# The last layer norm of a two-layer transformer: all loads ahead of the stores, scaling shared, last store halved

## The chip, the cores and the metric

The kernel runs on one core of a Trainium2 chip. A core has engines that run their own instruction streams and meet at semaphores: TensorE (PE: matmuls), VectorE (DVE), ScalarE (ACT), GpSimd (POOL) and SyncE (SP), which here only issues DMAs. DMAs move data between the chip's memory (HBM) and the on-chip memory (SBUF); they run on 16 DMA engines, and the issuing engine goes on without waiting for them. The metric is the device time of one execution in microseconds (us), the median of several runs.

## What is computed

Two post-norm transformer layers over 4 x 1024 tokens of width 256: attention and a gated feed-forward layer, then causal attention and a mixture of experts. Each of the four parts is added to its input and normalised. Cut to its end:

```python
def _layernorm(x, axis=-1, eps=1e-05):
    m = jnp.mean(x, axis=axis, keepdims=True)
    v = jnp.var(x, axis=axis, keepdims=True)
    return (x - m) / jnp.sqrt(v + eps)
...
x = _layernorm(x + _L0_attn_ref(x, ...))
x = _layernorm(x + _L0_ffn_ref(x, ...))
x = _layernorm(x + _L1_attn_ref(x, ...))
x = _layernorm(x + _L1_ffn_ref(x, ...))     # the experts; this norm is the last stage
return x
```

The change concerns the last of these norms only.

## The kernel before

Tokens are taken 128 at a time (a tile: 128 partitions, 256 numbers each); there are `NT` = 32 tiles. The two attention layers and the first feed-forward layer run in an order written out by hand. After them the kernel is in the hands of a planner, which orders each engine's instructions by itself, within the dependencies.

The mixture of experts accumulates in HBM: `acc_d` holds, for every token, the input of the last norm. The copy expert, the constant experts and the residual are written there first; then each of 12 experts (`EM`) computes four chunks of 128 rows and GpSimd adds them to `acc_d` with an indirect DMA (L1430). Expert e waits for the additions of expert e-1.

The last stage works in eight groups of `GRP` = 4 tiles. For each group:

- SyncE loads the group `xo` from `acc_d` (L1459, 512 KB, 4 KB for each partition). The loads depend on the additions of the last expert (`added[EM]`). `xo` has eight buffers, so no load waits for a buffer.
- VectorE computes mean and variance of each tile: `bn_stats` (L1465) and `bn_aggr` (L1466) into `mvo`.
- GpSimd makes `rs` = (variance + 1e-5) to the power -0.5 for the four tiles (L95, L96, in `inv_std`) and `sho` = -mean x `rs` (L1469, L1470).
- `finish` scales the tiles and stores the group to `out` (L1455, SyncE, 512 KB in rows of 1 KB). Tiles up to number 26 are scaled on ScalarE (L1454, `Identity` with scale `rs` and bias `sho`), the last five on VectorE (`normalise`, L100: subtract the mean, multiply by `rs`).

`finish` of a group is called one group late, after the statistics of the next one (`done`). In the planned order SyncE issues the loads of groups 0 to 4, the stores of 0 and 1, the load of 5, the stores of 2, 3 and 4, the load of 6, the store of 5, the load of 7, and the stores of 6 and 7. SyncE issues in order: a store that waits for its scaling holds what stands behind it.

Of the kernel before, what the change touches and what calls it, by code (L numbers as in the profile page):

```python
# [13 lines left out]
AF = mybir.ActivationFunctionType  # L14
# [5 lines left out]
P = 128  # L20
B, S, C = 4, 1024, 256
N = B * S
NT = N // P
# [12 lines left out]
def postln_layers_kernel(ctx: ExitStack, tc: tile.TileContext, a: dict, out: bass.AP):  # L36
    nc = tc.nc
# [10 lines left out]
        out=mask_h, in_=mask_h, pattern=[[-1, P]], compare_op=ALU.is_ge, fill=NEG, base=0, channel_multiplier=1  # L48
# [18 lines left out]
        out=before, in_=before, pattern=[[1, P]], compare_op=ALU.is_gt, fill=0.0, base=0, channel_multiplier=-1  # L67
# [24 lines left out]
    def inv_std(work, var, n, name, rs=None):  # L92
        if rs is None:
            rs = work.tile([P, n], F32, tag="rstd", bufs=4, name=f"rs_{name}")
        nc.gpsimd.tensor_scalar(rs, var, 1e-5, None, ALU.add)  # L95
        nc.gpsimd.tensor_tensor(rs, rs, neg_half.to_broadcast([P, n]), ALU.pow)  # L96
        return rs

    def normalise(x, mean, rs):
        nc.vector.tensor_scalar(x, x, mean, rs, ALU.subtract, ALU.mult)  # L100

    with ExitStack() as main:
# [65 lines left out]
        for s in range(2):  # L168
            k = float(D0) ** -0.5 if s == 0 else 1.0
# [1172 lines left out]
        st, tu, lo = route(3, True)  # L1342
# [45 lines left out]
    for e in range(EM):  # L1388
# [34 lines left out]
        for c in range(ECH):  # L1423
            py = ps_av.tile([P, 512], F32, tag="av", name=f"py_{e}_{c}")
            for f in range(FF1 // P):
# [5 lines left out]
                out=acc_d,  # L1431
# [12 lines left out]


    GRP = 4
    done = []

    def finish(x, mv, rs, sh, t0):
        for t in range(GRP):  # L1450
            if t0 + t >= NT - 5:
                normalise(x[:, t], mv[:, t, 0:1], rs[:, t : t + 1])
            else:
                nc.scalar.activation(x[:, t], x[:, t], AF.Identity, bias=sh[:, t : t + 1], scale=rs[:, t : t + 1])  # L1454
        nc.sync.dma_start(out[t0 * P : (t0 + GRP) * P, :].rearrange("(t p) d -> p t d", p=P), x)  # L1455

    for t0 in range(0, NT, GRP):
        x = mo.tile([P, GRP, C], F32, tag="xo", bufs=NT // GRP, name=f"xo_{t0}")
        ins = nc.sync.dma_start(x, acc_rows[:, t0 : t0 + GRP, :])  # L1459
        for other in added[EM]:  # L1460
            tc.add_manual_dep(ins.ins, other.name, must, reason="all experts' rows")
        mv = mo.tile([P, GRP, 2], F32, tag="mvo", bufs=4, name=f"mvo_{t0}")
        for t in range(GRP):
            st = mo.tile([P, 6], F32, tag="bnst", bufs=4, name=f"st_o_{t0 + t}")
            nc.vector.bn_stats(st, x[:, t])  # L1465
            nc.vector.bn_aggr(mv[:, t], st)  # L1466
        rs = inv_std(mo, mv[:, :, 1], GRP, f"o_{t0}")
        sh = mo.tile([P, GRP], F32, tag="sho", bufs=4, name=f"sho_{t0}")
        nc.gpsimd.tensor_scalar(sh, mv[:, :, 0], -1.0, None, ALU.mult)  # L1469
        nc.gpsimd.tensor_tensor(sh, sh, rs, ALU.mult)  # L1470
        done.append((x, mv, rs, sh, t0))
        if len(done) > 1:
            finish(*done.pop(0))
    finish(*done.pop())


# [61 lines left out]
```

## Time and profile before

| | us |
|---|---|
| median of 3 runs (2526.11 to 2530.27) | 2527.09 |
| the profiled execution | 2529.43 |
| its span, first to last instruction | 2527.6 |
| the last stage in it, from the first load of `xo` to the end | 39.0 (2488.6 to 2527.6) |

Busy time in the whole span and in the last stage:

| engine | span, us | last stage, us | instructions in the last stage |
|---|---|---|---|
| TensorE | 2364.4 | 0 | 0 |
| VectorE | 1364.7 | 15.2 | 69 |
| ScalarE | 1024.8 | 13.6 | 27 |
| GpSimd | 729.4 | 13.3 | 32 |
| DMA engines, mean share | | 62% at 215 GB/s | 16 DMAs of 512 KB |

The groups of instructions of the last stage, as the profile lists them (line, engine, operation, out<-in with shapes, count; busy us and mean ns of one; idle time of the engine just before them, and what ended it):

```profile
L1454 ACT ACTIVATE xo<-xo,sho,rs_o 128x256 f32<-128x256 f32 x27 | 13.6, 586 | 32.2 <-DVE st_o L1465 24.9 <-POOL sho L1470 7.3
L1465 DVE BATCH_NORM_STATS2 st_o<-xo 128x6 f32<-128x256 f32 x32 | 12.3, 402 | 19.0 <-DMA xo<-acc_d 19.0
L96 POOL TENSOR_TENSOR rs_o<-rs_o,neg_half 128x4 f32<-128x4 f32 x8 | 8.3, 1037 | 0.0
L1466 DVE BATCH_NORM_AGGREGATE mvo<-st_o 128x2 f32<-128x6 f32 x32 | 5.1, 169 | 0.0
L100 DVE TENSOR_SCALAR xo<-xo,mvo,rs_o 128x256 f32<-128x256 f32 x5 | 1.8, 409 | 3.5 <-POOL rs_o L96 3.5
```

An instruction may start before the one ahead of it on its engine has ended, so the time from one start to the next is shorter than a mean duration. Times in the text are us from the start of the span.

### The profile page before, as it was taken

The page shows a single profiled execution, that of the slowest core. Times are in us where ns is not written, and L with a number is a line of the kernel's source. Part 1 is how long each engine was busy: PE and PEld are TensorE (multiplying, and loading weights), DVE is VectorE, ACT ScalarE, POOL GpSimd, SP SyncE. Part 2 cuts the span into 40 slices and gives each one's busy share as a digit, 9 for nine tenths or more (in the row PEclk, how much of TensorE's full clock was granted, in tenths as well). Part 3 has the DMA queues.
Part 4 walks back from the last instruction along what each step waited for, and adds up shares of the span by engine and source line. Part 5 has one row for each costly group of instructions (what it writes and reads, how often), then busy time and mean ns, then how long its engine had stood idle before and what let it go on. Part 6 is the DMA issues. An engine that isn't in the chain of part 4 may idle for free.

```text
span 2527.6 us, 36682 instructions
## 1 busy us (share of the span) xinstructions
PE 2364.4 (94%) x14452; PEld 1194.9 (47%) x14452; DVE 1364.7 (54%) x3157; ACT 1024.8 (41%) x2015; POOL 729.4 (29%) x1015
## 2 busy tenths in 40 slices
PE   6999999999999999999999999999999983999993
PEld 3343334444445543444445434445566442666662
DVE  6765654766657447787563677817435654111112
ACT  1355554545552445545424455461331331111122
POOL 5633623425114122454121320211110143122213
PEclk8999999999998999999989999999998985999996
DMA  3034212000000000001000000112000012444434
GB/s 92 29 119 135 84 59 83 1 27 1 1 1 27 1 1 1 23 26 51 31 1 1 1 1 1 48 33 86 1 1 1 1 51 68 108 111 103 117 72 141
DMA packets 79612, 109.89 MB, mean 43 GB/s; under 512 B 8784, under 2 KB 68432, under 8 KB 77776
## 3 DMA queue, kind: packets, MB, share of 16 engines
q1 hardware_dynamic: 54336, 80.48, 9.8%
q0 software_dynamic: 9984, 14.82, 3.0%
q10 hardware_dynamic: 15120, 12.27, 1.7%
q8 instruction: 113, 1.85, 0.3%
q14 instruction: 59, 0.48, 0.1%
HBM read 68.64 MB, written 38.90 MB: 43 GB/s over the span
## 4 chain that ended last, share of the span: by engine, by line
PE 85%; DVE 8%; DMA 3%; POOL 2%; ACT 1%; issue 1%; SPq 0%; ACTq 0%; DVEq 0%; POOLq 0%
PE sc L458 19%; PE av L476 10%; PE ph L1410 7%; PE py L1426 7%; PE gu L595 7%; PE mx L434 4%; PE sc L978 4%; PE mx L931 4%; PE p L898 4%; PE dn L611 3%; PE av L1015 3%; PE dn L1015 2%; DVE part L942 2%; PE qk L298 2%; PE ppa L559 2%; PE pt L425 2%
## 5 line engine op out<-in xcount | busy, mean ns | idle before, releaser
L437 DVE TENSOR_REDUCE part<-mx 128x1 f32<-128x512 f32 x1024 | 656.5, 685 | 344.3 <-PE mx L434 338.6
L467 ACT ACTIVATE pe<-sc 128x512 f32<-128x512 f32 x1024 | 554.1, 596 | 394.5 <-PE mx L434 341.8
L434 PE MATMUL mx<-kT,qT 32*128 32x512 f32 x2048 | 650.3, 644 | 6.0 <-DVE part L437 5.7
L458 PE MATMUL sc<-qT,kT 32*128 32x512 f32 x2048 | 616.3, 638 | 0.2 <-ACT pe L467 0.2
L458 PEld LDWEIGHTS sc<-qT,kT 32*128 32x128 f32 x2048 | 182.1, 183 | 223.8 <-issue 177.7
L476 PE MATMUL av<-pe,va 128*32 128x512 f32 x2048 | 272.8, 605 | 0.0
L942 DVE TENSOR_REDUCE part<-mx 128x1 f32<-128x512 f32 (+3 forms) x384 | 186.9, 550 | 152.3 <-PE mx L940 108.6
L434 PEld LDWEIGHTS mx<-kT,qT 32*128 32x128 f32 x2048 | 196.6, 185 | 52.7 <-DVE part L437 27.4
L989 ACT ACTIVATE pe<-sc 128x512 f32<-128x512 f32 (+3 forms) x384 | 157.6, 499 | 156.4 <-PE sc L978 156.1
L1410 PE MATMUL ph<-dmT,f 128*128 128x512 f32 x384 | 170.3, 602 | 4.4 <-DVE dmT L90 3.5
L1426 PE MATMUL py<-f,hTm 128*128 128x256 f32 x768 | 167.7, 379 | 0.0
L1418 ACT ACTIVATE hTm<-ph,b 128x512 f32<-128x512 f32 x96 | 60.8, 684 | 261.3 <-PE ph L1410 261.3
L992 POOL TENSOR_SCALAR_AFFINE_SELECT pe<-pe 128x256 f32<-128x256 f32 x128 | 51.7, 411 | 374.6 <-ACT pe L989 372.4
L1426 PEld LDWEIGHTS py<-f,hTm 128*128 128x128 f32 x768 | 145.9, 190 | 25.0 <-issue 5.7
L1430 POOL DMA_INDIRECT acc_d<-yo,dm x48 | 74.5, 1552 | 284.9 <-DVE yo L1428 238.8
L931 PE MATMUL mx<-kT,qT 32*128 32x512 f32 (+3 forms) x768 | 138.6, 593 | 8.5 <-DVE part L942 4.8
L356 POOL TENSOR_TENSOR ss<-ss,neg_half 128x16 f32<-128x16 f32 x48 | 138.7, 2907 | 0.5
L1427 DVE TENSOR_TENSOR yo<-py,b 128x256 f32<-128x256 f32 x48 | 20.4, 425 | 207.6 <-PE py L1426 207.6
L476 PEld LDWEIGHTS av<-pe,va 128*32 128x32 f32 x2048 | 40.3, 108 | 193.9 <-issue 183.9
L978 PE MATMUL sc<-qT,kT 32*128 32x512 f32 (+3 forms) x768 | 117.9, 546 | 1.7 <-DVE part L942 0.6
L1410 PEld LDWEIGHTS ph<-dmT,f 128*128 128x128 f32 x384 | 72.9, 192 | 94.9 <-issue 86.7
L595 PE MATMUL gu<-xTf,wg 128*128 128x256 f32 x384 | 107.7, 403 | 0.0
(357 smaller groups left out, 2938.0 us busy)
## 6 DMA issues: line engine op xcount, KB each, us to landing
f<-in_fc SPq DMA_DIRECT2D x14, 1024.0 KB, 5.0
f<-in_fc ACTq DMA_DIRECT2D x10, 1024.0 KB, 6.0
xink<-in_xT SPq DMA_DIRECT2D x32, 256.0 KB, 2.8
disp_d<-empty SPq DMA_DIRECT2D x12, 520.0 KB, 5.1
qk_d<-xs SPq DMA_DIRECT2D x6, 1024.0 KB, 3.9
xr<-qk_d SPq DMA_DIRECT2D x6, 1024.0 KB, 6.5
dm<-disp_d SPq DMA_DIRECT2D x11, 520.0 KB, 3.7
xinv<-in_xT SPq DMA_DIRECT2D x16, 256.0 KB, 3.1
```

Source lines behind the costliest of these rows:

```text
L434: nc.tensor.matmul(sc, self.qT[r, t * P : (t + 1) * P], self.kT[r, u * 512 : (u + 1) * 512], start=True, stop=True)
L437: return lambda: nc.vector.tensor_reduce(self.part[:, t, u, h : h + 1], sc, AX.X, ALU.max, negate=True)
L458: nc.tensor.matmul(sc, self.m.kT[r, kt * P : (kt + 1) * P], self.m.qT[r, qb * 512 : (qb + 1) * 512], start=True, stop=True)
L467: nc.scalar.activation(self.pes[i, h // 2][:, h % 2, :], sc, AF.Exp)
L476: nc.tensor.matmul(self.av[32 * h : 32 * h + 32, :], va0[:, kt, 4 * self.g + h, :], self.pes[i, h // 2][:, h % 2, :], start=kt == 0, stop= ...
L595: nc.tensor.matmul(ps[:, i * 256 : (i + 1) * 256], w[:, c, f * P : (f + 1) * P], xT[j][:, c, :], start=c == 0, stop=c == 1,)
L931: nc.tensor.matmul(scs[h][:, :n], qT[r, t * P : (t + 1) * P], kT[r, u * 512 : u * 512 + n], start=True, stop=not diag,)
L942: nc.vector.tensor_reduce(self.part[:, t, u, h : h + 1], scs[h][:, :n], AX.X, ALU.max, negate=True)
L978: nc.tensor.matmul(scs[h][:, off:], ones_h[r, :] if w else kT[r, kt * P : (kt + 1) * P], (self.m.nmT if w else qT)[r, q], start=w == 0, st ...
L989: nc.scalar.activation(pe[:, j, off:], scs[2 * hp + j][:, off:], AF.Exp)
L1410: nc.tensor.matmul(ph[:, i * CAP : (i + 1) * CAP], f1[:, c, (f + i) * P : (f + i + 1) * P], dmT[:, c, :], start=c == 0, stop=c == 1,)
L1426: nc.tensor.matmul(py[:, :C], hT[:, f, c * P : (c + 1) * P], f2[:, f, :], start=f == 0, stop=f == FF1 // P - 1)
```

## The change

All eight loads are issued by a loop of their own ahead of the statistics and the stores. In `finish`, VectorE scales the last tile of each group, and in the last group tiles 1 and 3; ScalarE scales the others. The last group is stored in two halves of two tiles, the first from SyncE, the second from ScalarE's queue.

```diff
-    done = []
-
-    def finish(x, mv, rs, sh, t0):
-        for t in range(GRP):
-            if t0 + t >= NT - 5:
-                normalise(x[:, t], mv[:, t, 0:1], rs[:, t : t + 1])
-            else:
-                nc.scalar.activation(x[:, t], x[:, t], AF.Identity, bias=sh[:, t : t + 1], scale=rs[:, t : t + 1])
-        nc.sync.dma_start(out[t0 * P : (t0 + GRP) * P, :].rearrange("(t p) d -> p t d", p=P), x)
-
+    xo = []
     for t0 in range(0, NT, GRP):
         x = mo.tile([P, GRP, C], F32, tag="xo", bufs=NT // GRP, name=f"xo_{t0}")
         ins = nc.sync.dma_start(x, acc_rows[:, t0 : t0 + GRP, :])
         for other in added[EM]:
             tc.add_manual_dep(ins.ins, other.name, must, reason="all experts' rows")
+        xo.append(x)
+    done = []
+
+    def finish(x, mv, rs, sh, t0):
+        last = t0 + GRP == NT
+        for t in range(GRP):
+            if t == GRP - 1 or (last and t % 2):
+                normalise(x[:, t], mv[:, t, 0:1], rs[:, t : t + 1])
+            else:
+                nc.scalar.activation(x[:, t], x[:, t], AF.Identity, bias=sh[:, t : t + 1], scale=rs[:, t : t + 1])
+            if t % 2 and last:
+                lo = t0 + t - 1
+                eng = nc.sync if t == 1 else nc.scalar
+                eng.dma_start(out[lo * P : (lo + 2) * P, :].rearrange("(t p) d -> p t d", p=P), x[:, t - 1 : t + 1])
+        if not last:
+            nc.sync.dma_start(out[t0 * P : (t0 + GRP) * P, :].rearrange("(t p) d -> p t d", p=P), x)
+
+    for k, x in enumerate(xo):
+        t0 = k * GRP
         mv = mo.tile([P, GRP, 2], F32, tag="mvo", bufs=4, name=f"mvo_{t0}")
```

The rest of the loop (statistics, `rs`, `sho`, `finish` one group late) is as before. In the changed program the lines of the last stage are L1450 (loads), L1475 and L1476 (statistics), L1479 and L1480 (`sho`), L1462 (scaling on ScalarE), L1466 and L1468 (stores).

## The prediction

> **What bounds the kernel now.** I read the views from the whole to the end of it. The page gives PE 94% of the span, but the table of stages shows no matmul at all in the last 39.0 us: from 2488.6 to 2527.6 us VectorE is busy 15.2 us, ScalarE 13.6, GpSimd 13.3. The change touches only this stage, so I went to the chain of waits there.
>
> ```profile
> 2488.62 3.63 DMA xo<-acc_d
> ...
> 2500.06 0.39 SPq L1455
> 2500.50 5.71 DMA xo<-acc_d
> ...
> 2512.10 0.37 SPq L1455
> 2512.52 4.70 DMA xo<-acc_d
> ```
>
> Columns: start, length, what. Three loads of `xo` stand on the path, 14.0 us together, and the two later ones start the moment a store (L1455) has been issued. Why they start so late is in SyncE's timeline:
>
> ```profile
> 2488.62 2.25 SPq L1459 DMA_DIRECT2D xo<-acc_d  x5
> 2498.10 2.35 SPq L1455 DMA_DIRECT2D out<-xo  x2
> 2500.50 0.50 SPq L1459 DMA_DIRECT2D xo<-acc_d  x1
> 2502.03 4.30 SPq L1455 DMA_DIRECT2D out<-xo  x3
> 2506.38 0.51 SPq L1459 DMA_DIRECT2D xo<-acc_d  x1
> 2512.10 0.37 SPq L1455 DMA_DIRECT2D out<-xo  x1
> 2512.52 0.50 SPq L1459 DMA_DIRECT2D xo<-acc_d  x1
> 2516.94 5.60 SPq L1455 DMA_DIRECT2D out<-xo  x2
> ```
>
> The queue is in order: five loads go out at once, the sixth stands behind two stores, the seventh behind five, the eighth behind six, and each store waits for the scaling of its group. The table of waits puts the price on VectorE:
>
> ```profile
> DVE st_o L1465 <- DMA xo<-acc_d: 19.0, 4, 7.8
> ```
>
> Of these 19.0 us, 7.8 are the first load, which stays; the timeline gives the other three as 5.79, 3.58 and 1.77, so 11.1 us hang on the order of the queue.
>
> **The pace without those waits.** The timeline of the last group has every link of a turn:
>
> ```profile
> 2518.70 0.30 DVE L1466 BATCH_NORM_AGGREGATE mvo<-st_o 128x2 f32<-128x6 f32 x2
> 2519.16 0.23 POOL L95 TENSOR_SCALAR rs_o<-mvo 128x4 f32<-128x4 f32 x1 [3.86 <-DVE mvo L1466]
> 2519.49 0.23 POOL L1469 TENSOR_SCALAR sho<-mvo 128x4 f32<-128x4 f32 x1
> 2519.68 1.04 POOL L96 TENSOR_TENSOR rs_o<-rs_o,neg_half 128x4 f32<-128x4 f32 x1
> 2520.76 1.38 DVE L100 TENSOR_SCALAR xo<-xo,mvo,rs_o 128x256 f32<-128x256 f32 x4 [1.76 <-POOL rs_o L96]
> 2520.80 0.20 POOL L1470 TENSOR_TENSOR sho<-sho,rs_o 128x4 f32<-128x4 f32 x1
> ```
>
> While loads were in hand (the first five groups), three paces can be read from the timeline: VectorE takes 16 tiles in 6.49 us, 1.62 a group; ScalarE 20 scalings in 9.93 us, 0.49 each, 1.97 for four; GpSimd starts L95 at 2497.97 and again at 2499.87, 1.90 a group.
>
> **Part 1, loads ahead of all stores.** Eight issues of 0.45 to 0.50 us end about 2492.4; SyncE has nothing else until the first store, due 2497.6. At the 410 GB/s of the DMA row while the first five run, a 512 KB load takes 1.28 us, so the eighth lands about 2492.25 + 7 x 1.28 = 2501.2. Its statistics are due near 2508.9 (below): 7 us of cover. The stores now stand in the DMA rings behind the loads: the first would move from 2500.7 on. A store moves in 524 kB / 350 GB/s = 1.5 us and one is issued every 2.2 us, so this backlog is gone by the fourth. By itself this part would leave GpSimd's pace: the last `rs` at 2495.69 + 7 x 1.90 = 2509.0 (the first L96 ends at 2495.69), four L100 to 2510.4, the last store behind its forerunner landed about 2513.9, against 2525.1 now (issued 2522.16, 2.9 to landing). That is 11.2 us off.
>
> **Part 2, one tile in four on VectorE.** Seven groups move one scaling from ScalarE (0.49) to VectorE (0.32: four L100 in 1.38 less one of 0.41, over three). ScalarE falls to 1.48 a group, VectorE rises to 1.94. But the changed program's order on VectorE counts more: the scaling of group k-1 stands ahead of the last L1476 (aggregation; L1466 before) of group k. It waits for `rs` of k-1; the aggregation behind it is what L95 of group k waits for; and that makes `rs` of k. A ring is closed that was open before. One turn: `rs` to L100 0.04 (2520.72 to 2520.76), L100 0.32, aggregation 0.16, to L95 0.16 (2519.00 to 2519.16), L95 to the end of L96 1.56; sum **2.24 us**, over VectorE's 1.94 and GpSimd's 1.90. All VectorE work that is queued behind the waiting scaling (the aggregation and the next group's statistics) waits with it. The last `rs` ends at 2495.69 + 7 x 2.24 = 2511.4, so this part gives back 2.4 us.
>
> The bounds: not under 1.94 a turn (VectorE's work), not over 2.84 if each of the three GpSimd steps of the turn has to let half a 0.39 us statistics instruction pass. No row of before shows the ring; all its links have rows, so I take 2.24. A rule speaks against this part: the Trainium skill, "SBUF — State Buffer", section "Who interferes with whom", says that a VectorE instruction in a two-port mode and GpSimd exclude each other for the whole instruction. The row above disagrees: L1470 began 0.04 us into four L100 and took its usual 0.20. By the row it costs nothing; by the rule L1480 of the last group (L1470 before) would stand behind two scalings and end 0.7 us later, and so would everything after it. I keep the row.
>
> **Part 3, the last group.** Two tiles on ScalarE: `sho` is ready 0.28 after `rs`, ScalarE starts 0.03 later, the first scaling ends 0.58 later (2512.3), the second at 2512.76. Four L100 took 1.38 from 0.04 after `rs`, so this share is worth nothing; the gain is that a half can leave at 2512.3. The other half leaves from ScalarE's queue at 2512.8, where nothing stands behind it. A 256 KB store has no row: at most the 2.9 us of a 512 KB one, at least 2.2 (half of 1.5 less). Ahead of both is the seventh store: `rs` 2509.1, ScalarE to 2511.0, issued then, moving from about 0.95 us later to 2513.46. The two halves follow in another 1.5, to 2514.96, and landing is about 0.5 after the last packet (store of 2498.10: first packets 2499.0, landed 2501.0): 2515.5. One whole store at 2512.8 would land about 2515.8, so the halves bring 0.3.
>
> **Sum.** Last landing 2515.5 in place of 2525.1; the 2.5 us from landing to the end of the span stay. Span 2527.6 - 9.6 = 2518.0. Around the span the profiled execution has 2529.43 - 2527.6 = 1.8 us, so 2519.8 on its own terms. It was 2.3 us above the median of the runs shown; taken off the median, 2527.09 - 9.6 = **2517.5 us**. Nothing ahead of 2488 us changes its order on any engine.
>
> **Rivals.**
> - *The ring doesn't bind*: VectorE's work is the pace, 1.94 a turn. The last `rs` comes 2.1 us earlier: 2515.4. For it: VectorE waits only 0.3 us in each turn, so a little less latency opens the ring. Against: the order, and each link being measured. 0.12.
> - *The ring is slow*: 2.84 a turn, 4.2 us later, 2521.7. For it: the rule above, stretched to statistics instructions. Against: GpSimd kept 1.90 beside an unbroken row of statistics. 0.13.
> - *Slower: reads and writes together bind the stage.* The stage moves 8.39 MB; from 2502 to 2504, where a load ran among stores, the DMA engines were 90% busy at only 215 GB/s:
>
> ```profile
> 2502.00:2504.00 2.00, 0.00 (x0) 0.00 (x0) 0.00 (x0) 2.00 (x6) 1.43 (x4) 0.50 0.90 215
> 2504.00:2506.00 2.00, 0.00 (x0) 0.00 (x0) 0.00 (x0) 1.93 (x4) 0.00 (x0) 0.50 0.99 355
> ```
>
> (the last two columns are DMA share and GB/s). At 215 throughout, from the first packets at 2489.6, the last would move at 2528.6 and the median be 2531.1. It decides below 8.39 MB / 35.0 us = 240 GB/s. Against: two us later the same mix ran at 355, and now the loads come first and alone. 0.03.
> - *The loads don't go ahead after all*: the changed order on SyncE is eight loads, then the stores, and their waits are for transfers long done, so this has no more than 0.01.
>
> **How the numbers follow.** The forecast has 0.71. Faster than before by 0.2% is 5.05 us, about what a measurement of this kernel can tell from no change. The forecast and the open ring lie beyond it, the slow ring at 5.4 us is split by run noise (2526.11 to 2530.27 for one kernel): faster 0.88, same 0.09, slower 0.03. The range goes from the open ring less run noise, 2513.0, to the slow ring plus some, 2522.5.
>
> **What would show it.** In the changed trace: eight loads of `xo` in one row of SyncE, no wait of VectorE for a load but the first; L95 starting every 2.24 us (1.9 would open the ring); L100 ahead of each last aggregation with a short wait for `rs`; the last scaling near 2512.8. Loads landing later than 2505, or a VectorE wait for one of them, would make it wrong.

## The result

| | before | changed |
|---|---|---|
| median of 6 runs, us | 2526.56 (2523.58 to 2530.27) | 2517.04 (2514.16 to 2519.33) |
| profiled execution / its span, us | 2529.43 / 2527.6 | 2514.16 / 2512.3 |
| last stage, from the issue of the first load of `xo` to the end of the span, us | 39.0 | 29.4 |

The ratio is 0.9962, with a 95% interval from 0.9949 to 0.9975: 9.5 us off 2526.56. The two spans differ by 15.3 us, more than the change is worth: the stage is 9.6 us shorter, and what lies ahead of it ended 5.7 us earlier in this one execution. That second part is taken for run variation: the medians, 9.5 us apart, fit the stage alone, and the first two experiments show how far the start of the stage moves from run to run. From here on the stage is the measure.

The changed kernel's SyncE timeline (start, length, what):

```profile
2482.84 3.84 SPq L1450 DMA_DIRECT2D xo<-acc_d  x8
2491.74 13.62 SPq L1468 DMA_DIRECT2D out<-xo  x7
2506.28 0.37 SPq L1466 DMA_DIRECT2D out<-xo  x1
```

Eight loads in one row, then the stores. And its table of waits for the stage (who waited for whom: us in total, times, longest):

```profile
POOL rs_o L95 <- DVE mvo L1476: 10.4, 8, 7.7
DVE st_o L1475 <- DMA xo<-acc_d: 7.7, 1, 7.7
```

VectorE's waits for loads fell from four, 19.0 us, to the one that has to be. In their place GpSimd's addition L95 waits for an aggregation in every group, 7.7 us in the first and 0.3 to 0.4 in each of the others. One turn of the changed kernel's timeline shows why:

```profile
2494.20 0.41 DVE L100 TENSOR_SCALAR xo<-xo,mvo,rs_o 128x256 f32<-128x256 f32 x1 [0.16 <-POOL rs_o L96]
2494.25 0.20 POOL L1480 TENSOR_TENSOR sho<-sho,rs_o 128x4 f32<-128x4 f32 x1
...
2494.53 0.17 DVE L1476 BATCH_NORM_AGGREGATE mvo<-st_o 128x2 f32<-128x6 f32 x1
...
2494.80 0.23 POOL L95 TENSOR_SCALAR rs_o<-mvo 128x4 f32<-128x4 f32 x1 [0.35 <-DVE mvo L1476]
2495.11 0.23 POOL L1479 TENSOR_SCALAR sho<-mvo 128x4 f32<-128x4 f32 x1
...
2495.30 1.04 POOL L96 TENSOR_TENSOR rs_o<-rs_o,neg_half 128x4 f32<-128x4 f32 x1
...
2496.38 0.41 DVE L100 TENSOR_SCALAR xo<-xo,mvo,rs_o 128x256 f32<-128x256 f32 x1 [0.17 <-POOL rs_o L96]
```

Read it as a circle: L100 waits for L96, the aggregation stands behind L100 on VectorE, L95 waits for the aggregation, L96 follows L95. From L100 to L100 it is 2.18 us. L95 starts 2.17 to 2.24 us apart in all seven turns, and the last `rs` is ready 22.50 us after the first load was issued.

The end of the span has a row that the prediction did not use. The rows of the program's last line, in the kernel before (L1534) and in the changed one (L1544; count: shortest/median/longest in ns, first to last start):

```profile
L1534 POOLq DRAIN  x3: 46/102/6087, 2520.8 to 2527.4; - x3
L1534 SPq DRAIN  x3: 7/7/7, 2525.4 to 2527.1; - x3
L1544 POOLq DRAIN  x3: 46/102/6089, 2505.4 to 2512.0; - x3
L1544 SPq DRAIN  x3: 7/7/7, 2509.8 to 2511.7; - x3
```

In the changed kernel GpSimd's first DRAIN begins with its last step (2505.4) and takes 6.09 us, to 2511.5; the final exchange of semaphores follows it, and the span ends at 2512.3. SyncE, which waits for the stores, was ready at 2509.8. Before, it was the same: DRAIN to 2526.9, end at 2527.6, SyncE ready at 2525.4.

### The profile page after: what moved, and what is told of

Same layout as the page of the kernel before. It is cut to its first block, busy times and chain, and to the rows that moved or that the text cites. A ratio compares the mean times of both kernels' runs of the same rounds, so it can differ in the third digit from the quotient of the medians.

```text
span 2512.3 us, 36681 instructions
## 1 busy us (share of the span) xinstructions
PE 2360.3 (94%) x14452; PEld 1193.2 (47%) x14452; DVE 1366.7 (54%) x3161; ACT 1023.4 (41%) x2011; POOL 730.5 (29%) x1015
## 4 chain that ended last, share of the span: by engine, by line
PE 85%; DVE 8%; POOL 2%; DMA 2%; issue 1%; ACT 1%; SPq 0%; ACTq 0%; POOLq 0%; DVEq 0%
PE sc L458 19%; PE av L476 10%; PE ph L1410 7%; PE py L1426 7%; PE gu L595 7%; PE mx L434 4%; PE sc L978 4%; PE mx L931 4%; PE p L898 4%; PE dn L611 4%; PE av L1015 3%; PE dn L1015 2%; DVE part L942 2%; PE qk L298 2%; PE ppa L559 2%; PE pt L425 2%
```

## Experiments

All stages, in us after the issue of the first load of `xo` (its own start in the second column):

| kernel | first load | last `rs` | last landing | stage |
|---|---|---|---|---|
| before | 2488.6 | 32.1 | 36.5 | 39.0 |
| changed | 2482.8 | 22.5 | 26.6 | 29.4 |
| changed, again | 2484.1 | 22.5 | 26.6 | 29.4 |
| loads only | 2487.9 | 21.7 | 26.3 | 28.6 |
| loads only, again | 2482.7 | 20.8 | 25.4 | 27.7 |
| open ring | 2485.5 | 20.6 | 25.1 | 27.5 |
| whole last store | 2484.0 | 22.5 | 26.8 | 29.4 |
| power first | 2483.3 | 22.3 | 27.0 | 29.8 |
| no loads ahead | 2482.1 | 30.5 | 34.6 | 37.4 |
| power first, ScalarE scales | 2483.3 | 20.9 | 26.1 | 28.4 |
| power first, two tensors | 2485.5 | 21.1 | 25.4 | 28.3 |
| one more GpSimd step | 2484.2 | 22.7 | 26.8 | 30.7 |
| root in the last groups | 2485.7 | | 25.8 | 27.3 |

Two landings are estimates, since the traces lack them: those of the first profiles of the changed and the loads-only kernel. They are the end of the last packet and 0.3 us, as the second profile of the changed kernel has it.

### How far a profile repeats

> The changed kernel once more, for how far its profile repeats. The last stage (from the issue of the first load of xo to the end of the span) took 29.5 us in the changed kernel and 39.0 in the kernel before; what lies ahead of it ended 5.8 us earlier. If the change works only in the last stage and the 5.8 us are run noise, the stage is 29.5 +- 0.3 again and its start can be anywhere from 2480 to 2490 us. If the change also shortened what lies ahead, the stage starts at 2483 +- 1 again.

The stage was 29.4 us again and began at 2484.1, which hardly tells the two accounts apart. The loads-only kernel, profiled twice (below), does: it began its stage at 2487.9 and 2482.7. So the start of the stage moves by 5 us from run to run of one kernel, and in this pair the stage itself repeated within 0.1. A gain of 2 us is therefore out of reach of the medians here (their intervals are 3 to 4 us to each side) and plain in the stage.

### The loads ahead, and nothing else

`finish` as it was before, with the separate loop of loads:

```diff
-        last = t0 + GRP == NT
...
-            if t == GRP - 1 or (last and t % 2):
+            if t0 + t >= NT - 5:
...
-            if t % 2 and last:
-                lo = t0 + t - 1
-                eng = nc.sync if t == 1 else nc.scalar
-                eng.dma_start(out[lo * P : (lo + 2) * P, :]...)
-        if not last:
-            nc.sync.dma_start(out[t0 * P : (t0 + GRP) * P, :]...)
+        nc.sync.dma_start(out[t0 * P : (t0 + GRP) * P, :]...)
```

> The loads go ahead of the stores, the scaling and the last store stay as they were before. Theory of the ring: without a scaling of VectorE ahead of the last aggregation GpSimd's own pace of 1.90 us a group sets the last rs, about 20.6 us after the first load is issued; four scalings on VectorE and one whole store follow, last stage 27.8 us, 1.7 less than with all three parts. Rival, that sharing the scaling and halving the store carry part of the gain: over 29.5 us, with ScalarE's four scalings a group as the pace. The time of the whole against the kernel before: ratio about 0.9956 by the first, above 0.9962 by the rival, which a timed run can hardly tell apart; the stage does.

The stage was 28.6 us: below 29.5, but not 27.8. Its table of waits has one that does not belong there:

```profile
DVE st_o L1469 <- DMA xo<-acc_d: 8.9, 2, 7.8
```

Two waits instead of one: the third load was late. So the kernel was profiled again.

> The loads-only kernel once more. In its first profile the third load of xo was complete 8.15 us after the first was issued (6.1 in every other profile), VectorE waited 1.1 us for it and one turn took 2.84 us in place of 1.9; the last stage was 28.6. If that was a stray delay of one transfer: third load at 6.1 us, no wait of VectorE but the first, stage 27.7 +- 0.2. If it belongs to this kernel: the same delay again, 28.6.

This time the third load was in after 6.3 us, VectorE waited only for the first load, and the stage took 27.7 us. The delay did not come back. GpSimd's timeline in this second profile:

```profile
2492.08 0.23 POOL L95 TENSOR_SCALAR rs_o<-mvo 128x4 f32<-128x4 f32 x1
2493.99 0.23 POOL L95 TENSOR_SCALAR rs_o<-mvo 128x4 f32<-128x4 f32 x1
2495.88 0.23 POOL L95 TENSOR_SCALAR rs_o<-mvo 128x4 f32<-128x4 f32 x1
```

A turn is 1.9 us and L95 waits for nobody: GpSimd is the pace. Only the last turn takes 2.24 us, in both profiles. Tile 27 is scaled on VectorE in this kernel too, and it stands ahead of the last aggregation (L1470 here) of the last group, so the ring closes once, which the expectation left out:

```profile
2501.26 0.41 DVE L100 TENSOR_SCALAR xo<-xo,mvo,rs_o 128x256 f32<-128x256 f32 x1 [2.14 <-POOL rs_o L96]
...
2501.59 0.17 DVE L1470 BATCH_NORM_AGGREGATE mvo<-st_o 128x2 f32<-128x6 f32 x1
2501.92 0.23 POOL L95 TENSOR_SCALAR rs_o<-mvo 128x4 f32<-128x4 f32 x1 [0.42 <-DVE mvo L1470]
```

The loads alone take 11.3 us off the stage (10.4 with the late load), and the two other parts of the change give 1.7 back. Timed, this kernel stands to the one before as 0.9957 (0.9941 to 0.9974), which cannot be told from the change's 0.9962.

### The other two parts, and not the loads

The loop of the kernel before, with the `finish` of the change:

```diff
-    xo = []
     for t0 in range(0, NT, GRP):
         x = mo.tile([P, GRP, C], F32, tag="xo", ...)
         ins = nc.sync.dma_start(x, acc_rows[:, t0 : t0 + GRP, :])
...
-        xo.append(x)
...
-    for k, x in enumerate(xo):
-        t0 = k * GRP
```

> The scaling shared and the last store halved as in the change, but each load issued in its group as before, so that loads stand behind stores again (here the sixth behind four stores, the seventh and eighth behind five). If the loads are the gain: VectorE waits for loads again, the last three land about 21.5, 23 and 24.5 us after the first is issued, and the last stage takes about 36.4 us (35 to 38). If the two other parts were the gain: under 32 us.

37.4 us, inside what the theory of the loads gave. SyncE's timeline and the table of waits, which has the sixth load's wait of 4.7 us (12.4 less the 7.7 of the first):

```profile
2491.08 6.88 SPq L1461 DMA_DIRECT2D out<-xo  x4
2498.00 0.51 SPq L1465 DMA_DIRECT2D xo<-acc_d  x1
2499.83 0.37 SPq L1461 DMA_DIRECT2D out<-xo  x1
2500.24 1.79 SPq L1465 DMA_DIRECT2D xo<-acc_d  x2
```

```profile
DVE st_o L1471 <- DMA xo<-acc_d: 12.4, 2, 7.7
```

So 1.6 of the change's 9.6 us are there without its first part. The planner has put the stores and loads in another order here, three loads behind stores as before but two of them together; the 1.6 us are the worth of that order as much as of the sharing.

### The ring opened

One edge of order in the changed kernel: VectorE's scaling comes behind the last aggregation of the group whose statistics it stands among.

```diff
...
-                normalise(x[:, t], mv[:, t, 0:1], rs[:, t : t + 1])
+                ins = normalise(x[:, t], mv[:, t, 0:1], rs[:, t : t + 1])
+                tc.add_manual_dep(ins.ins, aggr[-1].name, after_it, reason="behind the last aggregation")
...
-            nc.vector.bn_aggr(mv[:, t], st)
+            aggr.append(nc.vector.bn_aggr(mv[:, t], st).ins)
```

> The changed kernel with one edge of order added: on VectorE each scaling comes behind the last aggregation of the next group, not ahead of it; same instructions, same engines. Theory of the ring: a turn falls from 2.2 us to the larger of GpSimd's 1.90 and VectorE's 1.94, the last rs comes 20.6 us after the first load is issued in place of 22.5, last stage 27.6 us. Rival, that the turn is set by the work of an engine or by the transfers and not by the order: L95 still starts every 2.2 us, stage 29.5.

27.5 us, with the last `rs` at 20.61. The timeline of two late turns:

```profile
2502.63 0.23 POOL L95 TENSOR_SCALAR rs_o<-mvo 128x4 f32<-128x4 f32 x1
...
2503.75 0.30 DVE L1479 BATCH_NORM_AGGREGATE mvo<-st_o 128x2 f32<-128x6 f32 x2
2504.21 0.41 DVE L100 TENSOR_SCALAR xo<-xo,mvo,rs_o 128x256 f32<-128x256 f32 x1 [0.16 <-POOL rs_o L96]
...
2504.54 0.23 POOL L95 TENSOR_SCALAR rs_o<-mvo 128x4 f32<-128x4 f32 x1
```

The aggregations (L1479 in this kernel) are done before L100 starts to wait, L95 waits for nothing and comes after 1.91 us, as in each of the last four turns. Same instructions, same transfers, another order: the ring was the pace. The timed ratio to the kernel before is 0.9952 (0.9935 to 0.9968), with a median of 2513.87 us.

### A link taken out of the ring, and what came in its place

GpSimd makes `rs` first and both steps of `sho` after it:

```diff
-        rs = inv_std(mo, mv[:, :, 1], GRP, f"o_{t0}")
...
+        nc.gpsimd.tensor_scalar(rs, mv[:, :, 1], 1e-5, None, ALU.add)
+        power = nc.gpsimd.tensor_tensor(rs, rs, neg_half.to_broadcast([P, GRP]), ALU.pow)
...
-        nc.gpsimd.tensor_scalar(sh, mv[:, :, 0], -1.0, None, ALU.mult)
+        ins = nc.gpsimd.tensor_scalar(sh, mv[:, :, 0], -1.0, None, ALU.mult)
+        tc.add_manual_dep(ins.ins, power.ins.name, after_it, reason="the power first")
         nc.gpsimd.tensor_tensor(sh, sh, rs, ALU.mult)
```

> The changed kernel with GpSimd's order in a group altered: rs first (addition, power), then both steps of sho, so the first step of sho no longer stands between the addition and the power. Same instructions. Theory of the ring: the turn loses that link (0.2 to 0.3 us), L95 comes every 1.95 to 2.05 us in place of 2.2, sho of the last group comes 0.3 us later; last stage 28.2 to 28.6 us. Rival, that GpSimd's work as such sets the turn: no change of the turn, 29.5 to 29.8.

The turn fell to 2.20 us only, and the stage grew to 29.8. These are the numbers of the rival, GpSimd's work as such, and not those of the ring. L95 waits for nobody in this kernel, so the ring is no longer the pace; but GpSimd's own work has become longer than its 1.90 us. The rows of `sho` (durations in ns: shortest/median/longest) say where:

```profile
L1482 POOL TENSOR_SCALAR sho<-mvo x8: 401/402/404, 2490.2 to 2505.6; 128x4 f32<-128x4 f32 x8
L1484 POOL TENSOR_TENSOR sho<-sho,rs_o x8: 198/199/255, 2490.7 to 2506.1; 128x4 f32<-128x4 f32 x8
```

The first step, 0.23 us in the changed kernel, takes 0.40 here, each time beside L100, and it ends 0.04 behind it. That agrees with the rule weighed in the prediction (the Trainium skill, "SBUF — State Buffer", section "Who interferes with whom"): one of the two is shut out while the other runs. Two runs test it.

> The power-first kernel, with all scaling but that of the last group on ScalarE. With power first, the first step of sho on GpSimd (L1482) ran beside VectorE's scaling (L100) and took 0.40 us in all eight groups, ending with L100; elsewhere the same step took 0.23. Theory of the lock (VectorE's scaling shuts GpSimd's step out): 0.23 us in the first seven groups, 0.40 in the last, and a turn of 2.03 to 2.05 us in place of 2.20. Rival, that the step is slower because of what GpSimd ran just ahead of it (the power): 0.40 in all groups, turn 2.20.

```diff
-            if t == GRP - 1 or (last and t % 2):
+            if last and t % 2:
```

GpSimd's timeline with VectorE's scaling gone from the first seven groups:

```profile
2494.16 0.24 POOL L1482 TENSOR_SCALAR sho<-mvo 128x4 f32<-128x4 f32 x1
2494.48 0.20 POOL L1484 TENSOR_TENSOR sho<-sho,rs_o 128x4 f32<-128x4 f32 x1
2494.77 0.23 POOL L1479 TENSOR_SCALAR rs_o<-mvo 128x4 f32<-128x4 f32 x1
2495.07 1.04 POOL L1480 TENSOR_TENSOR rs_o<-rs_o,neg_half 128x4 f32<-128x4 f32 x1
2496.18 0.24 POOL L1482 TENSOR_SCALAR sho<-mvo 128x4 f32<-128x4 f32 x1
```

0.24 us in seven groups, 0.40 in the last, where two L100 run beside it; a turn of 2.02 to 2.05. So it is VectorE's scaling that makes the step long, not the power ahead of it. This order of GpSimd's steps is simply its own work, one after the other; the order of the changed kernel hides L1479 between the addition and the power.

> The power-first kernel, with the first step of sho on GpSimd as a product of two tensors (by a constant -1 tile) in place of a product with a number, still beside VectorE's scaling. In the changed kernel a two-tensor step of GpSimd (L1480) began in the same place beside L100 and kept its 0.20 us. If it is the kind of step that decides who is shut out: about 0.20 us beside L100, turn 2.00 to 2.05 us. If any GpSimd step there is shut out: about 0.40 us, turn 2.20.

```diff
...
-        ins = nc.gpsimd.tensor_scalar(sh, mv[:, :, 0], -1.0, None, ALU.mult)
+        ins = nc.gpsimd.tensor_tensor(sh, mv[:, :, 0], neg_one.to_broadcast([P, GRP]), ALU.mult)
```

A turn of this kernel's timeline (L102 is VectorE's scaling here):

```profile
2494.16 0.20 POOL L1484 TENSOR_TENSOR sho<-mvo,neg_one 128x4 f32<-128x4 f32 x1
2494.22 0.41 DVE L102 TENSOR_SCALAR xo<-xo,mvo,rs_o 128x256 f32<-128x256 f32 x1
2494.43 0.25 POOL L1486 TENSOR_TENSOR sho<-sho,rs_o 128x4 f32<-128x4 f32 x1
```

The two-tensor step kept 0.20 us in all eight groups, and six of the seven turns were 1.98 to 2.05 us, as expected; the last took 2.35, which is not explained. But the step began 0.05 to 0.06 us ahead of L102, where the product with a number had begun 0.05 behind the scaling, so the run does not tell the kind of step from the order of starting. The step behind it, also of two tensors and begun 0.21 us after L102, took 0.25 in place of 0.20, and ended 0.06 behind L102, so two tensors alone do not spare a step. Against the order alone speaks L1480 of the changed kernel: it began 0.04 us after L100 in all eight groups and kept its 0.20. What spares it stays open.

### The last store in one piece

```diff
-            if t % 2 and last:
-                lo = t0 + t - 1
-                eng = nc.sync if t == 1 else nc.scalar
-                eng.dma_start(out[lo * P : (lo + 2) * P, :]...)
-        if not last:
-            nc.sync.dma_start(out[t0 * P : (t0 + GRP) * P, :]...)
+        nc.sync.dma_start(out[t0 * P : (t0 + GRP) * P, :]...)
```

> The changed kernel with the last group stored whole from SyncE. By the prediction's account the halves bring 0.3 us: stage 29.8. Rival, that the half on ScalarE's queue costs at the end of the program (from the last landing to the end of the span it was 2.85 us, 2.5 before) as much as it brings: stage 29.4 to 29.5, with 2.5 us from the landing to the end. If a store's time were all fixed cost, the whole store would land with the second half: 29.4.

The last landing came 0.2 us later, and the stage was no longer: 29.37 against 29.42. The prediction's 29.8 is out, and so is the third account, since the landing moved. The numbers of the second came true (29.4, with 2.5 us behind the landing), but the rows of the last line point to another reason:

```profile
L1539 POOLq DRAIN  x3: 46/102/6089, 2506.5 to 2513.1; - x3
L1539 SPq DRAIN  x3: 7/7/7, 2511.1 to 2512.9; - x3
```

GpSimd's DRAIN runs from 2506.5 to 2512.6, and SyncE is ready at 2511.1: there is 1.5 us of room on SyncE's side. If the end waits for GpSimd, the halves shorten what nobody waits for. The next two runs test that.

### Who ends the span

One more step on GpSimd behind the last group's `sho`, into a tile that is not read:

```diff
+        if t0 + GRP == NT:
+            more = mo.tile([P, GRP], F32, tag="more", bufs=1, name="more")
+            nc.gpsimd.tensor_tensor(more, rs, neg_half.to_broadcast([P, GRP]), ALU.pow)
```

> The changed kernel with one more power on GpSimd behind the last group's sho, into a tile that nobody reads. In every profile so far GpSimd's last row is a DRAIN of 6.09 us that starts with its last instruction, and the span ends 0.79 us after it: 6.88 us after GpSimd's last step, whatever the stores do. If that drain sets the end: GpSimd's last step comes 1.1 us later, the last landing stays at 26.6 us after the first load is issued, and the stage takes 30.5 (29.4 + 1.1). Rival, that the end follows the last landing at a distance of 2.3 to 2.9 us: 29.4.

```profile
L1547 POOLq DRAIN  x3: 46/102/7121, 2507.0 to 2514.6; - x3
```

The stage grew by 1.2 us to 30.65 (0.2 of it from a first load that came in later), with the last landing at 26.8. The end follows GpSimd. Then the other way round: on top of the open ring, `rs` and `sho` of the last two groups are made without GpSimd.

```diff
...
+        if t0 < NT - 2 * GRP:
...
+        else:
...
+            nc.scalar.activation(rs, mv[:, :, 1], AF.Sqrt, bias=eps)
+            nc.vector.reciprocal(rs, rs)
+            nc.vector.scalar_tensor_tensor(sh, mv[:, :, 0], -1.0, rs, ALU.mult, ALU.mult)
...
```

> The open-ring kernel, with rs and sho of the last two groups made without GpSimd (square root on ScalarE, reciprocal and product on VectorE; the table for the root is loaded behind group 0), so that GpSimd is done two groups earlier, about 17.1 us after the first load is issued. If GpSimd's drain set the end: its drain ends at 23.2, the end is now set by the last landing (about 25.4, the root and ScalarE's scaling stand in one queue) and SyncE's and the other engines' 1.2 us behind it: stage 26.6 us, 0.9 less than the open ring. If the end always follows a landing at 2.3 to 2.9 us: 27.9 to 28.2, more than the open ring. Against the kernel before: ratio about 0.995.

```profile
L1558 POOLq DRAIN  x3: 46/102/6087, 2502.5 to 2512.4; - x3
L1558 SPq DRAIN  x3: 7/7/7, 2511.8 to 2512.1; - x3
```

GpSimd's long DRAIN now begins at 2502.5 and is over at 2508.6. SyncE is the last, at 2511.8, and the span ends 1.5 us after the last landing; in every other kernel that distance was 2.3 to 3.9 us. The stage is 27.3 us, the shortest of all, though not the 26.6 expected: the end stood 1.5 us behind the last landing and not 1.2, and the landing came at 25.8 and not 25.4. The root of group 6 stands in ScalarE's queue behind the scaling of group 5; with it the seventh store, and the last landing behind it, came 0.7 us later than in the open ring. (ScalarE's table load for the root, 1.28 us, stood ahead of the stage, at 2468.1, and cost it nothing.) Timed: 0.9956 (0.9939 to 0.9973), median 2514.66.

Loads only, open ring and root all beat the kernel before, and all have a shorter stage than the change, by 1.7 to 2.1 us (loads only with its late load by 0.8). In the whole time their intervals overlap with the change's.

## Why the prediction was right

- **The queue was the bound, and the loads were the gain.** Shown: the loads alone brought 11.3 us of the stage and 11.1 of the last landing (11.2 in the prediction), the rest without them 1.6 of the stage. The issues took 3.84 us, and in the second profile of the changed kernel the eighth load was complete after 12.5 us (12.6), and the first four stores landed 4.9, 4.0, 3.2 and 2.9 us after their issue: the backlog behind the loads was gone by the fourth.
- **The ring.** Its turn was 2.22 us on average against 2.24, its last `rs` at 22.5 us against 22.8. The rival without a ring, 1.94 a turn, and the slow ring, 2.84, are both out: the turn did not fall between them by chance, since one edge of order brought 1.91, and the one turn of the loads-only kernel that has the ring took 2.24.
- **What the second and third part give back, right by luck.** 1.6 us of the last landing in the sum. Measured were 1.7 us of the stage, but only 1.2 of the last landing (25.4 against 26.6). On the last `rs` the ring was to cost 2.4 us and cost 1.7 (20.8 against 22.5): the pace of 1.90 for the loads alone left out the one turn that tile 27 closes.
- **The rule of the shared port.** For this change the row was right: L1480 took 0.20 us beside L100 in all eight groups. But the row stood for that step only. The rule does act in this stage: a product with a number, put in the same place, lost 0.17 us a turn.
- **Reads and writes together.** The transfers of the stage ran at 332 GB/s from the first to the last (239 before). The rival, no gain or a loss, needed this rate to stay below 240; it is out. But reads and writes hardly ran together: the loads came in 1.28 us apart, the eighth at 12.5 us, and the first store, issued at 8.9, landed at 13.8. What a long mix of both moves was not put to the test.
- **The halves, wrong.** Forecast 0.3 us; the last landing came 0.2 earlier for them, and the end not at all.
- **The end, right by two errors.** "The 2.5 us from landing to the end of the span stay" was the wrong step. The last landing came 9.9 us earlier, not 9.6, and the distance to the end grew to 2.8 us. What ends the span in both kernels is GpSimd's DRAIN, which starts with its last step, and the 0.79 us of final exchange behind it, 6.88 us together; that step moved from 32.2 to 22.6 us after the first load, by 9.6. The number held because the last step and the last store both follow the last group's `rs`, and so moved by nearly the same.

## What to carry to other kernels

Read the order of an issuing queue before the waits of the engines: a load that stands behind a store waits for the whole computation of that store. When work is spread to an idle engine, look at what is queued behind it there; a wait for another engine's result, put ahead of that engine's next input, makes the latency of both the pace, and one edge of order can undo it. And before shortening the last store, find the row that the end of the program waits for; it need not be the store.

## What the hardware showed that I had not expected

- GpSimd's DRAIN at the end of the program took 6.09 to 6.15 us, and 7.12 where one more power (1.08 us) ran under it. One figure covers all 13 profiles: it ended 5.85 us after GpSimd's last step had ended, whatever that step was and wherever the stores stood. In all but that of the root in the last groups the span ended 0.79 us after it. What it waits for stays open.
- A GpSimd product with a number, 128x4, took 0.40 us beside VectorE's scaling and 0.23 to 0.24 elsewhere; the product of two tensors L1480 of the changed kernel, begun as shortly after the scaling, kept 0.20.
- In one of two profiles of the same kernel one load of 512 KB was complete about 2 us late, and all behind it were late too. It cost the stage 0.9 us. Its cause stays open.
